# Pairwise complex sums with a lag of three, host-made masks and an FFN product in parts, in a Toeplitz-attention kernel on one core

## The chip, the cores and the metric

The kernel runs on one core of a Trainium2 chip. The metric is the device time of one execution in microseconds (us), lower is better. Before the change three runs gave 678.74, 679.80 and 680.02 us; their median, 679.8 us, is the time to beat. All data are float32.

The core has five instruction streams, each executed in its own order: TensorE (PE, matmuls; its weight loads are listed as PEld), VectorE (DVE), ScalarE (ACT), GpSimd (POOL) and SyncE (SP), which here only issues DMA transfers.

## The reference, cut to what matters

`x` has shape (4, 2048, 256). Two residual blocks follow one another.

```python
# block 1: gated Toeplitz operator
n  = layernorm(x)
u, v = split(silu(n @ uv_w), 2)              # 256 channels each
a  = rpe(lags) * 0.99 ** abs(lags)           # 4-layer network of width 32, one value per lag and channel
y  = irfft(rfft(a) * rfft(v))[:, :2048]      # convolution along the 2048 positions
x  = x + (u * y) @ o_w
# block 2: grouped linear layers without a nonlinearity between them
h1 = einsum('gmh,goh->gmo', layernorm(x).reshape(8, 1024, 256), W1) + b1
x  = x + einsum('gmo,gho->gmh', h1, W2) + b2 # 8 groups of 1024 tokens
```

## The kernel before, in words

**The convolution.** The long convolution of 4096 points is split by polynomial remainders into 8 rings, `r = 0` to 7. One *unit* is one batch `b` and one half `h` of 128 channels; there are 8 units. For each unit, `prepare` (L515, `split_real` and `split_complex`) forms the eight remainders from `c` by VectorE additions. `stage_b` (L545) then runs over the rings:

- `forward(r)` (L556) loads a 256 KB matrix (`ring_mats`), transforms the remainder by four 128x256 matmuls into the PSUM tile `pf`, and multiplies it as complex numbers by the kernel's transform `am`: `y = pf * a` (L574), `far = swapped pf * a2` (L576), then real parts subtracted (L577) and imaginary parts added (L578). The last two read two SBUF tiles; each covers 128 partitions by 256 elements.
- `backward(r)` (L580) loads the matrix of the way back and multiplies `y` into the PSUM tile `acc` (L591).
- `after(r)` (L597) combines the rings, two at a time.

`step(r)` (L679) does `forward(r)` and then `backward` and `after` of ring `r - LAG`, with LAG = 2, so that a unit takes 10 steps. `y` has three buffers of 128x512, `far` one, `pf` and `acc` two PSUM buffers each. Between the steps the main loop (L739) interleaves pieces of other work: `end()` of the previous unit (the last additions, the four sums `tk` of L674 and the multiplications by the gate on GpSimd, L676), `prepare` of the next unit from step 5 on, and, by `between`, whole stages of the neighbouring work.

**The other stages.** `stage_a(b, q)` (L254) normalizes and transposes 512 tokens, multiplies by `uv_w` and lets GpSimd build `c` (L274, L276). `gate` (L537) computes `u`. `stage_d(b, q)` (L689) multiplies by `o_w` (`po`, L697), adds to `x` (L699), normalizes, multiplies by the FFN matrix (`pff`, L715), adds (L717) and stores. Since the two FFN layers have nothing between them, `stage_w(g)` (L480) multiplies the two weight matrices of group `g` into one 256x256 matrix: four chunks of two 256 KB loads each, through two buffers for each matrix (WB = 2), a bias put in by ScalarE (L498), 16 matmul instructions into `pw` (L502), and one VectorE instruction for `wt` (L510). The groups 0 to 3 are formed before the units, 4 to 6 in one call after step 1 of the units (2,0), (2,1) and (3,0), and group 7 after the last unit.

**The start.** `rpe_network` (L299) evaluates the small network on all lags at once with block-diagonal weights. Its masks are made on the chip: `blk` (which of four blocks a partition belongs to) is a VectorE reduction of the identity matrix (L310), the block-diagonal weights `bd` (L317, three instructions) and the first layer's weights `w0` (L321) are products with `blk` and with a corner of the identity. The first matmul of the network (L332) needs `w0` and the row `lag_t`. Each layer goes PE (`ph`), ACT (square and copy), PE (variance, L341), DVE (`inverse_root`, nine to twelve small instructions, then L347), PE (transposes, L350), DVE (L351), ACT (L353). Then `rpe_transform` makes the transforms `am` (matmuls `hp` L453 and `pa` L458).

**What sets the order.** The kernel is written in a framework that traces the calls as written, gives each instruction a priority by that order, and then fixes one order for each engine by itself, from priorities, data dependences and free buffers; it also places the semaphores. An edit can thus move instructions that it doesn't name. Both builds' orders can be listed engine by engine.

Of the kernel before, what the change touches and what calls it, by code (L numbers as in the profile page):

```python
# [42 lines left out]
F, L = 32, 3  # L43
# [4 lines left out]
NR = 7  # L48
WB = 2
PIECES = 3  # L50
LAG = 2
WT = 4
D_STEPS = ((4, 0), (5, 1), (5, 0), (6, 2), (6, 1), (7, 3), (7, 2), (8, 3))
PI = 3.141592653589793
# [7 lines left out]
def kernel(  # L62
# [41 lines left out]
    am_d = const.tile([P, 2, 3, 2, P], F32, name="amd")  # L104
    am_c = [const.tile([P, 2, 2, 2, P], F32, name=f"am{r}") for r in range(NR)]

    BUFS = {"f4": 2, "f2": 2, "ring": 6, "y": 3, "far": 1, "i4": 4, "i2": 5}

    def t4(name, tag):
        return work.tile([P, 8 * P], F32, tag=tag, bufs=BUFS[tag], name=name)  # L110

    def t2(name, tag):
        return work.tile([P, 4 * P], F32, tag=tag, bufs=BUFS[tag], name=name)

    def load_x(b, q, tag):
# [181 lines left out]
        return t, y  # L297

    def rpe_network():  # L299
        par = t4("par", "f4")[:, : 2 * (L + 1) + (L + 1) * F]  # L300
        nc.sync.dma_start(par, rpe_par)
        lnw, lnb = par[:, 0 : L + 1], par[:, L + 1 : 2 * L + 2]
        fcw = par[:, 2 * L + 2 :].rearrange("p (l f) -> p l f", f=F)
        lag_t = t4("lag_t", "i4")
        nc.sync.dma_start(lag_t[0:4, :], lag_rows)
        early.update({(0, q): load_x(0, q, "xa") for q in range(2)})
        decay = t4("decay", "f4")[:, :NT]
        nc.sync.dma_start(decay, decays)
        blk = const.tile([P, 4], F32, name="blk")
        V.tensor_reduce(blk, ident.rearrange("p (s f) -> p s f", f=F), AX.X, ALU.add)  # L310
        mean = small.tile([P, L + 1], F32, tag="rmean", name="rmean")
        V.tensor_reduce(mean, fcw, AX.X, ALU.add)
        V.tensor_scalar_mul(mean, mean, 1.0 / F)
        V.tensor_tensor(fcw, fcw, mean[:, :, None].to_broadcast([P, L + 1, F]), ALU.subtract)
        bd = t2("bd", "f2")[:, : L * 4 * F].rearrange("p (l s f) -> p l s f", l=L, f=F)
        for i in range(L):
            V.tensor_tensor(  # L317
                bd[:, i], fcw[:, i : i + 1, :].to_broadcast([P, 4, F]), blk[:, :, None].to_broadcast([P, 4, F]), ALU.mult
            )
        w0 = t2("w0", "f2")[0:4, : 4 * F].rearrange("p (s f) -> p s f", f=F)  # L320
        V.tensor_tensor(  # L321
            w0, fcw[0:4, L : L + 1, :].to_broadcast([4, 4, F]), ident[0:4, 0:4, None].to_broadcast([4, 4, F]), ALU.mult
        )
        V.tensor_scalar_mul(blk, blk, 1.0 / F)

        zs = [None, None]
        for i in range(L + 1):
            sqs, ds = [], []
            for k in range(2):
                ph = ps_f.tile([P, 4 * P], F32, tag="pf", name=f"ph{i}_{k}")  # L330
                if i == 0:
                    T.matmul(ph, w0.rearrange("p s f -> p (s f)"), lag_t[0:4, k * 4 * P : (k + 1) * 4 * P], start=True, stop=True)  # L332
                else:
                    T.matmul(ph, bd[:, i - 1].rearrange("p s f -> p (s f)"), zs[k], start=True, stop=True)
                sqs.append(t2(f"sq{i}_{k}", "i2"))
                A.activation(sqs[k], ph, AF.Square)
                ds.append(t2(f"d{i}_{k}", "y"))
                A.copy(ds[k], ph)
            pv = ps_i.tile([P, 8, 4], F32, tag="acc", name=f"pvar{i}")
            for c in range(8):  # L340
                T.matmul(pv[:, c, :], sqs[c // 4][:, c % 4 * P : (c % 4 + 1) * P], blk, start=True, stop=True)  # L341
            t, y = inverse_root(pv.rearrange("p c s -> p (c s)"), NT, f"{i}")
            for k in range(2):

                e = t2(f"ne{i}_{k}", "i2")
                t_, y_ = (a[:, k * 16 : (k + 1) * 16, None].to_broadcast([P, 16, F]) for a in (t, y))
                V.scalar_tensor_tensor(e.rearrange("p (n f) -> p n f", f=F), t_, 1.5, y_, ALU.add, ALU.mult)  # L347
                pr = ps_i.tile([P, 4 * P], F32, tag="acc", name=f"pr{i}_{k}")
                for c in range(4):
                    T.transpose(pr[:, c * P : (c + 1) * P], e[:, c * P : (c + 1) * P], ident)  # L350
                V.tensor_tensor(ds[k], ds[k], pr, ALU.mult)  # L351
                zs[k] = t2(f"z{i}_{k}", "i2")
                A.activation(zs[k], ds[k], AF.Silu, bias=lnb[:, i : i + 1], scale=lnw[:, i : i + 1])  # L353
# [125 lines left out]

    def stage_w(g):  # L480
        na, oc = INTER // P, 2

        b1t = small.tile([P, 3, na], F32, tag="b1", bufs=2, name=f"b1_{g}")
        nc.sync.dma_start(b1t, b1[g])
# [7 lines left out]
        for o in range(0, na, oc):  # L492
# [6 lines left out]
            for m in range(2):  # L499
                for a in range(oc):  # L500
# [5 lines left out]
                        start=(o + a + m == 0),  # L506
                        stop=(o + a == na - 1 and m == 1),
                    )
        wt = wts[g] = tok.tile([P, 2, D], F32, tag="wt", bufs=WT, name=f"wt_{g}")
        V.scalar_tensor_tensor(wt, row[:, None, :].to_broadcast([P, 2, D]), 0.5, pw, ALU.mult, ALU.add)  # L510

# [32 lines left out]

    def stage_b(b, h):  # L545
        rs = rings[b, h]
        ys, accs = {}, {}
        nm = f"{b}_{h}"

        def i4(name):  # L550
# [5 lines left out]
        def forward(r):  # L556
            m = ring_mats(r, 0, f"{nm}_{r}")
            pf = ps_f.tile([P, 2, 2, P], F32, tag="pf", name=f"pf_{nm}_{r}")
            for k in range(2):
                cols = slice(k * P, (k + 1) * P)  # L560
                for xx in range(2):
                    if r == 0:
                        T.matmul(pf[:, k, xx, :], m[:, xx, cols], rs[r][:, k, xx, :], start=True, stop=True)
                    else:
                        T.matmul(pf[:, k], m[:, xx, cols], rs[r][:, :, xx, :], start=(xx == 0), stop=(xx == 1))  # L565
            y = ys[r] = t2(f"y_{nm}_{r}", "y").rearrange("p (k r c) -> p k r c", k=2, r=2)
            f = t2(f"far_{nm}_{r}", "far").rearrange("p (k r c) -> p k r c", k=2, r=2)
            if r == 0:
                a = am_d[:, h]
                V.tensor_tensor(y, pf, a[:, 0:2].rearrange("p r k c -> p k r c"), ALU.mult)  # L570
# [3 lines left out]
                V.tensor_tensor(y, pf, a[:, 0, :, None, :].to_broadcast([P, 2, 2, P]), ALU.mult)  # L574
                a2 = a[:, 1]
            V.tensor_tensor(f, pf[:, :, ::-1, :], a2[:, :, None, :].to_broadcast([P, 2, 2, P]), ALU.mult)  # L576
            V.tensor_tensor(y[:, :, 0, :], y[:, :, 0, :], f[:, :, 0, :], ALU.subtract)  # L577
            V.tensor_tensor(y[:, :, 1, :], y[:, :, 1, :], f[:, :, 1, :], ALU.add)  # L578

        def backward(r):  # L580
            m, y = ring_mats(r, 1, f"{nm}_{r}"), ys.pop(r)
# [6 lines left out]
            else:  # L588
                for c in range(2):
                    for k in range(2):  # L590
                        T.matmul(  # L591
                            acc[:, c].rearrange("p x c -> p (x c)"), y[:, k, c, :], m[:, k, :], start=(k == 0), stop=(k == 1)
                        )

        st = {}

        def after(r):  # L597
            acc = accs.pop(r)
# [126 lines left out]
    z = rpe_network()  # L725
    for q in range(NQ):
        stage_a(0, q)
    stage_w(0)
    stage_w(1)
    for h in range(2):  # L730
        gate(0, h)
    phs = load_phases()
# [1 line left out]
    for _ in prepare(0, 0):  # L734
        pass
    for g in range(2, WT):
        stage_w(g)
    end = None
    for b in range(B):  # L739
        for h in range(2):  # L740
# [10 lines left out]
                for q in range(NQ):  # L751
                    between[1 + q].append(lambda b=b, q=q: stage_a(b + 1, q))
            if WT <= 2 * b + h < 2 * B - 1:
                between[1].append(lambda g=2 * b + h: stage_w(g))
            queue = [end()] if end else []
            nxt = 2 * b + h + 1
            for r in range(NR + 1 + LAG):
# [9 lines left out]
    gate(B - 1, 1)  # L767
    for _ in end():
        pass
    stage_w(2 * B - 1)  # L770
    quarters = [stage_d(B - 1, q) for q in range(NQ)]
    for q in range(NQ + 1):
        if q < NQ:
# [104 lines left out]
```

## Time and profile before

| what | value |
|---|---|
| median of three runs | 679.8 us |
| the profiled execution, its own time | 680.03 us |
| its span, first to last instruction | 678.2 us (1.8 us lie around it) |
| mean granted TensorE clock | 0.975 |
| PE busy | 595.7 us, 88% |
| PEld busy | 463.1 us, 68% |
| DVE busy | 522.1 us, 77%, 1164 instructions |
| ACT busy | 303.4 us, 45% |
| POOL busy | 163.7 us, 24% |
| DMA | 81.36 MB, mean 120 GB/s |
| chain that ended last | DVE 35%, PE 34%, ACT 12%, DMA 7%, POOL 6% |

How to read it: the busy shares are averages over stages that have different limits, so the page alone doesn't say what one stage is worth. The profile can be cut into windows of time, in which each engine's busy time is listed (a window in which one engine is busy all the time is set by that engine), and it lists for each instruction the start, the duration, and the idle time of its engine just before it with the event that ended it. Units of the main loop can be found by their first forward matmuls (L563): 114.7, 211.5, 428.5 and 577.8 us are some of them. From the batch 1 on one batch takes 147 us (345 to 492 us is one such stretch).

### The profile page before, as it was taken

The page shows a single profiled execution, that of the slowest core. Times are in us where ns is not written, and L with a number is a line of the kernel's source. Part 1 is how long each engine was busy: PE and PEld are TensorE (multiplying, and loading weights), DVE is VectorE, ACT ScalarE, POOL GpSimd, SP SyncE. Part 2 cuts the span into 40 slices and gives each one's busy share as a digit, 9 for nine tenths or more (in the row PEclk, how much of TensorE's full clock was granted, in tenths as well). Part 3 has the DMA queues.
Part 4 walks back from the last instruction along what each step waited for, and adds up shares of the span by engine and source line. Part 5 has one row for each costly group of instructions (what it writes and reads, how often), then busy time and mean ns, then how long its engine had stood idle before and what let it go on. Part 6 is the DMA issues. An engine that isn't in the chain of part 4 may idle for free.

```text
span 678.2 us, 8266 instructions
## 1 busy us (share of the span) xinstructions
PE 595.7 (88%) x2620; PEld 463.1 (68%) x2620; DVE 522.1 (77%) x1164; ACT 303.4 (45%) x774; POOL 163.7 (24%) x186
## 2 busy tenths in 40 slices
PE   3989898899898789998997799898995999999897
PEld 1767455788677677765786687756784777766676
DVE  3554794579988998884469998981399999898854
ACT  3677641213341226668811155768711066511143
POOL 2333010001562231015521420134410311130310
PEclk9999999899898899999998999998999899999899
DMA  8423734664232523441245423431345223431202
GB/s 257 155 86 93 178 101 150 167 211 149 89 125 81 181 82 114 127 171 63 78 140 155 125 63 124 149 139 37 119 136 174 64 86 138 147 124 32 62 33 93
DMA packets 39988, 81.36 MB, mean 120 GB/s; under 512 B 5636, under 2 KB 7172, under 8 KB 39944
## 3 DMA queue, kind: packets, MB, share of 16 engines
q1 hardware_dynamic: 39208, 79.91, 38.2%
q10 hardware_dynamic: 736, 0.92, 0.4%
q8 instruction: 21, 0.34, 0.2%
q14 instruction: 23, 0.19, 0.1%
HBM read 72.42 MB, written 8.39 MB: 119 GB/s over the span
## 4 chain that ended last, share of the span: by engine, by line
DVE 35%; PE 34%; ACT 12%; DMA 7%; POOL 6%; issue 5%; SPq 0%; POOLq 0%; DVEq 0%; ACTq 0%
PE acc L591 6%; PE pff L715 5%; DMA w<-in_L_ffn_W_dram 5%; PE pf L565 4%; PE pw L502 4%; PE pv L268 4%; ACT junk_d L138 3%; DVE far L576 3%; ACT xn_d L161 2%; DVE y L574 2%; PE pa L458 2%; DVE tk L674 2%; PE pu L542 2%; DVE y L578 2%; POOL rs_d L140 2%
## 5 line engine op out<-in xcount | busy, mean ns | idle before, releaser
L591 PE MATMUL acc<-mats,y 128*128 128x256 f32 x448 | 107.8, 380 | 1.9 <-issue 1.2
L591 PEld LDWEIGHTS acc<-mats,y 128*128 128x128 f32 x448 | 84.0, 190 | 14.7 <-issue 2.4
L502 PE MATMUL pw<-w,w 128*128 128x256 f32 x256 | 70.9, 422 | 20.4 <-DMA w<-in_L_ffn_W_dram 19.4
L502 PEld LDWEIGHTS pw<-w,w 128*128 128x128 f32 x256 | 52.1, 211 | 34.9 <-ACT w L498 19.4
L676 POOL TENSOR_TENSOR gt<-gt,tk 128x512 f32<-128x512 f32 x32 | 47.4, 1505 | 110.3 <-DVE tk L674 100.9
L498 ACT ACTIVATE w<-w,dw 128x256 f32<-128x256 f32 x64 | 29.2, 500 | 92.7 <-DMA w<-in_L_ffn_W_dram 90.4
L697 PE MATMUL po<-ow,gt 128*128 128x256 f32 x256 | 61.3, 385 | 5.0 <-POOL gt L676 5.0
L268 PE MATMUL pv<-uvw,xnt 128*128 128x256 f32 x256 | 62.9, 396 | 2.1 <-ACT xnt L174 2.0
L565 PE MATMUL pf<-ra,mats 128*128 128x256 f32 x256 | 62.5, 380 | 1.2 <-PE acc L591 1.2
L715 PE MATMUL pff<-wt,xn 128*128 128x256 f32 x256 | 59.6, 383 | 1.3 <-ACT xn L172 1.3
L268 PEld LDWEIGHTS pv<-uvw,xnt 128*128 128x128 f32 x256 | 48.9, 197 | 13.1 <-ACT xnt L174 6.4
L697 PEld LDWEIGHTS po<-ow,gt 128*128 128x128 f32 x256 | 48.5, 193 | 13.7 <-POOL gt L676 7.4
L542 PE MATMUL pu<-xnt,uvw 128*128 128x512 f32 x128 | 56.7, 592 | 0.0
L715 PEld LDWEIGHTS pff<-wt,xn 128*128 128x128 f32 x256 | 47.4, 190 | 10.3 <-ACT xn L172 3.7
L615 ACT COPY e<-acc 128x512 f32<-128x512 f32 x24 | 13.9, 580 | 88.9 <-PE acc L591 54.6
L565 PEld LDWEIGHTS pf<-ra,mats 128*128 128x128 f32 x256 | 47.5, 190 | 7.7 <-PE acc L591 1.9
L274 POOL TENSOR_TENSOR c<-v 128x256 f32<-128x256 f32 x32 | 33.1, 1033 | 78.8 <-ACT v L269 78.8
L574 DVE TENSOR_TENSOR y<-pf,am 128x512 f32<-128x512 f32 x56 | 38.3, 684 | 9.5 <-PE pf L565 9.5
L161 ACT ACTIVATE xn_d<-xd,nb_d,rs_d 128x256 f32<-128x256 f32 x56 | 29.1, 590 | 32.5 <-POOL nb_d L142 21.2
L542 PEld LDWEIGHTS pu<-xnt,uvw 128*128 128x128 f32 x128 | 24.2, 190 | 25.9 <-issue 23.0
L140 POOL TENSOR_TENSOR rs_d<-ve_d,mhalf 128x4 f32<-128x4 f32 x12 | 14.1, 1173 | 112.2 <-DVE ve_d L139 112.2
L565 PE MATMUL pf<-rb,mats 128*128 128x256 f32 x128 | 35.2, 413 | 6.0 <-issue 5.1
(198 smaller groups left out, 1141.3 us busy)
## 6 DMA issues: line engine op xcount, KB each, us to landing
mats<-in_mats_dram SPq DMA_DIRECT2D x128, 256.0 KB, 2.7
w<-in_L_ffn_W_dram SPq DMA_DIRECT2D x64, 256.0 KB, 4.4
xa<-in_x_dram SPq DMA_DIRECT2D x18, 512.0 KB, 3.3
xd<-in_x_dram SPq DMA_DIRECT2D x14, 512.0 KB, 3.5
out_dram<-xd SPq DMA_DIRECT2D x12, 512.0 KB, 2.6
mats_rpe<-in_mats_dram SPq DMA_DIRECT2D x8, 256.0 KB, 3.7
row<-in_L_ffn_b_dram SPq DMA_DIRECT2D x8, 128.0 KB, 4.5
ph<-in_phases_dram SPq DMA_DIRECT2D x4, 256.0 KB, 6.1
```

What stands on the lines that cost most here:

```text
L161: A.activation(xn[:, i, :], xt[:, t, :], AF.Identity, bias=nb[:, t : t + 1], scale=rstd[:, t : t + 1])
L268: T.matmul(pv[:, hf, :], xnt[:, dt, o : o + P], uvw[:, dt, D:], start=(dt == 0), stop=(dt == 1))
L274: G.tensor_tensor(c[:, r, j0 : j0 + 2, 0, :], hi, lo, ALU.add)
L498: A.activation(w1s[:, a, :], w1s[:, a, :], AF.Identity, bias=d[:, o + a : o + a + 1])
L502: T.matmul(pw[:, m, :], w1s[:, a, m * P : (m + 1) * P], w2s[:, a, :], start=(o + a + m == 0), stop=(o + a == na - 1 and m == 1),)
L542: T.matmul(pu, uvw[:, dt, h * P : (h + 1) * P], xnts[b, q][:, dt, :], start=(dt == 0), stop=(dt == 1))
L565: T.matmul(pf[:, k], m[:, xx, cols], rs[r][:, :, xx, :], start=(xx == 0), stop=(xx == 1))
L574: V.tensor_tensor(y, pf, a[:, 0, :, None, :].to_broadcast([P, 2, 2, P]), ALU.mult)
L591: T.matmul(acc[:, c].rearrange("p x c -> p (x c)"), y[:, k, c, :], m[:, k, :], start=(k == 0), stop=(k == 1))
L676: G.tensor_tensor(gs, gs, tk, ALU.mult)
L697: T.matmul(po[:, i, :], gts[b, h][:, 2 * q + j, i, :], ow[:, h, :], start=(h == 0), stop=(h == 1))
L715: T.matmul(pf[:, i, :], xn2[:, dt, o : o + P], wt[:, dt, :], start=(dt == 0), stop=(dt == 1))
```

## The change

1. **Sums by pairs.** `y` and `far` become tiles for two rings (128x1024). The products of an even ring go to the first half, those of the odd ring to the second; only after the odd ring one subtraction and one addition, of 512 elements each, do the sums of both. `y` has two such pair buffers in place of three single ones, `far` one.
2. **A lag of three.** LAG goes from 2 to 3, so that `backward(r)` comes a step later and a unit has 11 steps.
3. **Masks from the host.** `blk` and the corner of the identity come as 8 more columns of the parameter array `par`; the reduction L310 goes, and `w0` is made ahead of `bd`.
4. **The FFN product in parts.** `stage_w` becomes a generator. For the groups 4 to 6 its four chunks follow after the steps 1 to 4 and `wt` after step 5. For the other groups all parts are still run at once.

```diff
-LAG = 2
+LAG = 3
...
-    BUFS = {"f4": 2, "f2": 2, "ring": 6, "y": 3, "far": 1, "i4": 4, "i2": 5}
+    BUFS = {"f4": 2, "f2": 2, "ring": 6, "y": 2, "far": 1, "i4": 4, "i2": 5}
...
     def t2(name, tag):
+        if tag in ("y", "far"):
+            return t4(name, tag)[:, : 4 * P]
...
     def rpe_network():
-        par = t4("par", "f4")[:, : 2 * (L + 1) + (L + 1) * F]
+        nw = 2 * (L + 1) + (L + 1) * F
+        par = t4("par", "f4")[:, : nw + 8]
...
-        blk = const.tile([P, 4], F32, name="blk")
-        V.tensor_reduce(blk, ident.rearrange("p (s f) -> p s f", f=F), AX.X, ALU.add)
+
+        blk, seg = par[:, nw : nw + 4], par[:, nw + 4 :]
         mean = small.tile([P, L + 1], F32, tag="rmean", name="rmean")
...
+        w0 = t2("w0", "f2")[0:4, : 4 * F].rearrange("p (s f) -> p s f", f=F)
+        V.tensor_tensor(
+            w0, fcw[0:4, L : L + 1, :].to_broadcast([4, 4, F]), seg[0:4, :, None].to_broadcast([4, 4, F]), ALU.mult
+        )
         bd = t2("bd", "f2")[:, : L * 4 * F].rearrange("p (l s f) -> p l s f", l=L, f=F)
...
-        w0 = t2("w0", "f2")[0:4, : 4 * F].rearrange("p (s f) -> p s f", f=F)
-        V.tensor_tensor(
-            w0, fcw[0:4, L : L + 1, :].to_broadcast([4, 4, F]), ident[0:4, 0:4, None].to_broadcast([4, 4, F]), ALU.mult
-        )
...
     def stage_w(g):
         na, oc = INTER // P, 2
+        yield
...
                         stop=(o + a == na - 1 and m == 1),
                     )
+            yield
         wt = wts[g] = tok.tile([P, 2, D], F32, tag="wt", bufs=WT, name=f"wt_{g}")
...
     def stage_b(b, h):
...
-            y = ys[r] = t2(f"y_{nm}_{r}", "y").rearrange("p (k r c) -> p k r c", k=2, r=2)
-            f = t2(f"far_{nm}_{r}", "far").rearrange("p (k r c) -> p k r c", k=2, r=2)
+
+            if r % 2 == 0:
+                st["y"], st["f"] = (
+                    t4(f"{t}_{nm}_{r}", t).rearrange("p (n k r c) -> p n k r c", n=2, k=2, r=2) for t in ("y", "far")
+                )
+            ypair, fpair = st["y"], st["f"]
+            y, f = ypair[:, r % 2], fpair[:, r % 2]
+            ys[r] = y
...
-            V.tensor_tensor(y[:, :, 0, :], y[:, :, 0, :], f[:, :, 0, :], ALU.subtract)
-            V.tensor_tensor(y[:, :, 1, :], y[:, :, 1, :], f[:, :, 1, :], ALU.add)
+            if r % 2:
+                for part, op in ((0, ALU.subtract), (1, ALU.add)):
+                    yp = ypair[:, :, :, part, :].rearrange("p n k c -> p (n k) c")
+                    fp = fpair[:, :, :, part, :].rearrange("p n k c -> p (n k) c")
+                    V.tensor_tensor(yp, yp, fp, op)
...
             if WT <= 2 * b + h < 2 * B - 1:
-                between[1].append(lambda g=2 * b + h: stage_w(g))
+                w = stage_w(2 * b + h)
+                for r in range(6):
+                    between[r].append(lambda w=w: next(w, 0))
...
-    inputs = {**inputs, "rpe_par": np.tile(par, (4, 1))}
+    eye = np.eye(P, 4)
+    inputs = {**inputs, "rpe_par": np.concatenate([np.tile(par, (4, 1)), np.repeat(np.eye(4), F, axis=0), eye], axis=1).astype(par.dtype)}
```

More of the change, by code (lines that the diff above doesn't have):

```diff
@@ L299, in rpe_network @@
     def rpe_network():
-        par = t4("par", "f4")[:, : 2 * (L + 1) + (L + 1) * F]
+        nw = 2 * (L + 1) + (L + 1) * F
+        par = t4("par", "f4")[:, : nw + 8]
         nc.sync.dma_start(par, rpe_par)
         lnw, lnb = par[:, 0 : L + 1], par[:, L + 1 : 2 * L + 2]
-        fcw = par[:, 2 * L + 2 :].rearrange("p (l f) -> p l f", f=F)
+        fcw = par[:, 2 * L + 2 : nw].rearrange("p (l f) -> p l f", f=F)
         lag_t = t4("lag_t", "i4")
@@ L546, in stage_b @@
         rs = rings[b, h]
-        ys, accs = {}, {}
+        ys, accs, st = {}, {}, {}
         nm = f"{b}_{h}"
@@ L593, in backward @@
                         )
-        st = {}
         def after(r):
@@ L727 @@
         stage_a(0, q)
-    stage_w(0)
-    stage_w(1)
+    for g in range(2):
+        list(stage_w(g))
     for h in range(2):
@@ L736 @@
     for g in range(2, WT):
-        stage_w(g)
+        list(stage_w(g))
     end = None
@@ L769 @@
         pass
-    stage_w(2 * B - 1)
+    list(stage_w(2 * B - 1))
     quarters = [stage_d(B - 1, q) for q in range(NQ)]
```

## The prediction

> **What bounds the kernel now.** I read the page's busy rows first (PE 88%, DVE 77%, so neither alone), then cut one batch into windows. Columns: window, its length, then busy us of PE, PEld, DVE, ACT, POOL.
>
> ```profile
> 206.70:245.30 38.60, 30.52 (x130) 25.07 (x129) 38.60 (x73) 5.18 (x11) 10.46 (x8) 0.91 0.46 136
> 245.30:292.00 46.70, 43.16 (x210) 35.98 (x208) 42.75 (x94) 29.18 (x87) 8.70 (x10) 1.00 0.36 114
> 345.00:391.00 46.00, 37.56 (x164) 30.96 (x163) 46.00 (x97) 5.54 (x12) 13.02 (x8) 0.93 0.48 138
> 391.00:458.00 67.00, 62.91 (x277) 47.44 (x276) 61.29 (x126) 42.70 (x125) 14.58 (x15) 1.00 0.36 120
> 458.00:492.00 34.00, 30.77 (x139) 23.74 (x138) 8.37 (x18) 26.23 (x71) 14.88 (x22) 0.95 0.23 78
> ```
>
> From the first `st` of a batch to the last `tk` (345 to 391 us) VectorE is busy 46.00 of 46.00: it alone sets that stretch. From there to the gate's end PE is busy 62.91 of 67 and VectorE 61.29: PE leads, with about 4 us of waits. Then 34 us of PE and ACT in which VectorE does 8 us. So a VectorE saving counts in the first stretch, little in the second, nothing in the third.
>
> The timeline of the first 24 us, VectorE, then PE:
>
> ```profile
> 4.08 0.29 DVE L314 TENSOR_TENSOR par<-par,rmean 128x128 f32<-128x128 f32 x1
> 6.99 0.76 DVE L147 BATCH_NORM_STATS2 st_a<-xa 128x6 f32<-128x256 f32 x2 [2.62 <-DMA xa<-in_x_dram]
> ...
> 9.37 0.27 DVE L310 TENSOR_REDUCE blk<-ident 128x4 f32<-128x128 f32 x1
> ...
> 10.42 0.69 DVE L317 TENSOR_TENSOR bd<-par,blk 128x128 f32<-128x128 f32 x3
> 11.03 0.28 DVE L321 TENSOR_TENSOR w<-par,ident 4x128 f32<-4x128 f32 x1
> ```
> ```profile
> 11.36 3.78 PE L332 MATMUL ph<-lag_t,w 4*128 4x512 f32 x4 [11.36 <-DMA w<-in_L_ffn_W_dram]
> 15.07 1.87 PE L341 MATMUL pvar<-blk,sq 128*128 128x4 f32 x8
> 16.80 1.52 PE L170 MATMUL pt_a<-ident,xn_a 128*128 128x128 f32 x6
> 18.11 1.71 PE L341 MATMUL pvar<-blk,sq 128*128 128x4 f32 x8
> 19.68 0.67 PE L170 MATMUL pt_a<-ident,xn_a 128*128 128x128 f32 x2
> ```
>
> PE does nothing for 11.36 us. The row names a weight load, but `ph` doesn't read it: it reads `w0`, which ends at 11.31. VectorE idles from 4.37 to 6.99 and makes `w0` only after the statistics of two `xa` tiles. From 11.36 on PE is busy 8.99 of 8.99 and then 42.96 of 45.65 us (to 66).
>
> **The masks.** The reduction (0.27) goes; 8 columns (4 KB on 68 KB) cost nothing. In the changed build's VectorE order `w0` stands fourth, right after L314: it ends at 4.37 + 0.3 = 4.7. The other operand, `lag_t`, was issued at 1.2; the loads behind it show that it has landed by 5.7. So `ph` starts at 5.0 to 5.7, and `ph` and `pvar` (3.78 + 3.4 us) end at 12.2 to 12.9, just as the normalized tokens come (ACT L161, 10.53 to 12.61). The first eight transposes (2 us) end near 14.6, in place of 20.35: a lead of 5.7 us. The matmuls are the same, and PE is nearly full afterwards, so most of it lasts. What could eat it: ScalarE now squares `ph` before it normalizes (two pairs of 0.6 us behind the end of `ph` at 8.8 to 9.5, done by 10.7, covered), PE has less other work between the transposes of layer one, and from 58 us the w ring, two buffers with 4.4 us a load, sets the pace: the chain of waits has weight loads at 66.00 and 74.33. A load is released by the matmuls before it, so the ring shifts as a whole; the changed PE order ends the second chunk about 1 us of matmul work later. From below 0, from above 7; I take 5.0, near what the timeline gives.
>
> **The sums.** The rows of the adds, all shapes apart:
>
> ```profile
> L578 DVE TENSOR_TENSOR y<-y,far 128x256 f32<-128x256 f32 x64 | 35.2, 550 | 0.0
> ...
> L577 DVE TENSOR_TENSOR y<-y,far 128x256 f32<-128x256 f32 x64 | 31.1, 486 | 0.3
> ```
>
> 128 instructions of 256 elements become 64 of 512. Back to back the timeline shows a start every 0.334 us for 256 elements (L577 to L578, 360.93 and 361.26) and every 0.600 us for 512. A merged one saves 2 x 0.334 - 0.600 = 0.068 us: 64 x 0.068 = 4.3 us, over all stages. [...]
>
> The means of 486 and 550 against medians of 418 and 419 are waits for GpSimd, 12.8 us together:
>
> ```profile
> 387.84 0.42 DVE L609 TENSOR_TENSOR s<-td,acc 128x256 f32<-128x256 f32 x1
> 388.17 0.57 DVE L577 TENSOR_TENSOR y<-y,far 128x256 f32<-128x256 f32 x1
> 388.66 1.48 DVE L578 TENSOR_TENSOR y<-y,far 128x256 f32<-128x256 f32 x1
> 390.07 0.41 DVE L610 TENSOR_TENSOR s<-td,acc 128x256 f32<-128x256 f32 x1
> ```
>
> GpSimd's gate product runs from 386.87 to 389.86; the add that reads PSUM (L609) passes, the two that read SBUF twice wait. [...] by the rows it is the adds that wait. In the new order one pair of adds still stands right behind the first two `tk`, the other pair some 3.8 us behind the second two, past the product. I take a gain of 1.5 us; ends -3 (a loss) and +6.
>
> **The lag and the order.** I added up the spacings along both builds' VectorE orders. From a batch's first `st` to its last `tk` the work falls from 35.8 to 33.6, 45.0 to 42.6 and 45.6 to 42.6 us, 7.7 in all: the block behind `after(3)` moves past it. PE pays part back. From the first `po` that needs the second gate to the gate's end its order holds 67.9 in place of 66.6 us (one `backward`, 1.73, now comes after that point), +1.3; the third time the end is another, and I take the same; +0.4 in the stage after it. So 7.7 - 3 x 1.7 = 2.6 us. The moved `po` additions may let the 4 us of waits of the second stretch shrink; that is inside the range. The units (0,0) and (0,1): 0.5 us. Against: after the last unit's seventh product two backwards instead of one are left, and the new PE order puts 2.1 us more before the last `acc`, on the chain of `end`, GpSimd and `po` that closes at 640.8: +1.6 us.
>
> **Buffers.** A pair buffer is written again when both its backwards are done: `y(4)` waits for `acc(1)`, `y(6)` for `acc(3)`, which PE has behind `po` batches (3.2 us). Behind it on VectorE wait sums and the `xd` additions that `po` and the normalization need. In the 46 us stretch PE is ahead (37.56 of 46), in the next PE is the bound anyway. Taken at 0; up to 1.73 to 4.9 us a time.
>
> **FFN parts.** The same 48 matmul instructions and 24 loads. PE now stands still up to 4 us for a load (370.87: 4.08; 224.87: 3.69), but inside the stretch that VectorE fills: covered, 0. If VectorE no longer covered it, it would be about 4 us three times. On SP the loads stand among ring matrices; with three buffers each these are early. Ends -2 and +3.
>
> **Sum.** 5.0 + 1.5 + 2.6 + 0.5 - 1.6 = 8.0, and 0.3 of plain spacing gain in other VectorE-bound stretches: 8.3. The profiled execution took 680.03 us (span 678.2 and 1.8 around it), 0.2 above the median: 680.0 - 8.3 = 671.7, for the median 671.5 us.
>
> **Rivals.** (A) The w ring keeps its own time and the head start is lost: 679.8 - 3.3 = 676.5. For it: two of the start's waits on the chain are weight loads. Against: they are released by PE's own matmuls. (B) A head start of 7, all 7.7 us of VectorE without PE paying, and 2 us of the second stretch's waits gone: 679.8 - 7 - 7.7 - 2 - 0.5 + 1.6 = 664.2. Against: PE is 94% busy there. (C) Slower: the pair buffers. 16 times (`y(4)` and `y(6)` in eight units) VectorE stands for a backward that PE has behind `po`. At 1 us each it costs 16 and gives 679.8 + 16 - 8.3 = 687.5; it decides from 8.3 / 16 = 0.5 us each. Against: PE has slack where VectorE is the bound.
>
> **Chances.** Main case 0.57, its own range 667.5 to 675; A 0.20, of which 0.05 ends within 0.2% of before (1.4 us, about what a measurement of this kernel can tell from no change); B 0.15; C 0.08. Faster 0.57 + 0.15 + 0.15 = 0.87, same 0.05, slower 0.08. The range 665 to 678.5 leaves out C, the best of B and the end of A.
>
> **What would show it.** Right: `ph` at 5 to 5.7 us, `hp` near 85 instead of 90.14; 64 adds of 128x512 with a median near 690 ns; the stretch from `st` to the last `tk` shorter by 2 to 3 us with VectorE still full; the next one not shorter than 66. Wrong: `hp` still at 90 (A); idle before L574's successor with `acc` as releaser (C); PE waits below 2 us in the second stretch (B).

## The result and the profile after

The changed kernel takes 675.86 us, median of 15 runs (673.67 to 680.34), against 679.8 us before (15 runs beside them): ratio 0.9938, 95% interval 0.9917 to 0.9958, a gain of 4.2 us (2.9 to 5.6) where 8.3 were foretold. Its profiled execution took 674.42 us with a span of 672.6 us; before it was 678.2, so 5.6 us separate the two traces. The mean granted TensorE clock (the share of its full clock that TensorE gets) is 0.975 in both traces; over all 15 runs of the changed kernel it is 0.971, over the 30 runs of the kernel before that stand beside the first experiments 0.979.

The start is as foretold. Timeline of the first microseconds after, PE and then VectorE:

```profile
5.64 3.75 PE L335 MATMUL ph<-lag_t,w 4*128 4x512 f32 x4 [5.64 <-DVE par L327]
9.32 3.58 PE L344 MATMUL pvar<-par,sq 128*128 128x4 f32 x16
12.75 1.95 PE L172 MATMUL pt_a<-ident,xn_a 128*128 128x128 f32 x8
```
```profile
4.18 0.29 DVE L317 TENSOR_TENSOR par<-par,rmean 128x128 f32<-128x128 f32 x1
4.51 0.28 DVE L319 TENSOR_TENSOR w<-par 4x128 f32<-4x128 f32 x1
```

`w0` ends at 4.79 and `ph` starts at 5.64; the first eight transposes are done at 14.7. `hp` starts at 84.3 us (90.1 before).

Next, the stages of the loop. Windows after, then the one window of before that the prediction did not show (length, busy us of PE, PEld, DVE, ACT, POOL, then the clock, the DMA share and GB/s):

```profile
199.80:236.90 37.10, 28.08 (x124) 22.29 (x123) 37.10 (x65) 4.59 (x11) 7.41 (x9) 0.95 0.48 135
236.90:304.40 67.50, 63.46 (x276) 47.75 (x275) 53.67 (x113) 45.58 (x134) 13.71 (x14) 1.00 0.37 123
304.40:340.80 36.40, 30.38 (x148) 25.14 (x146) 12.86 (x24) 24.27 (x65) 17.17 (x23) 0.95 0.26 82
340.80:386.60 45.80, 37.02 (x158) 30.03 (x157) 45.65 (x89) 4.74 (x10) 7.16 (x9) 0.89 0.42 126
386.60:453.70 67.10, 63.27 (x277) 47.83 (x276) 54.77 (x116) 45.55 (x134) 14.16 (x14) 1.00 0.35 120
453.70:488.60 34.90, 29.79 (x144) 24.17 (x142) 11.81 (x22) 23.93 (x64) 17.48 (x23) 0.95 0.23 78
```
```profile
312.00:344.90 32.90, 29.05 (x138) 22.68 (x137) 8.09 (x18) 26.07 (x71) 14.61 (x21) 1.00 0.24 80
```

VectorE still fills the first stretch (37.10 of 37.10; 45.65 of 45.80), but the third, from the gate's end to the next `st`, has grown from 32.90 to 36.40 us, and VectorE's work in it from 8.09 to 12.86.

Cutting every trace at the same events (first `st` of a batch, end of its last `tk`, end of the gate's matmuls `pu`) gives the ledger. V is the stretch from `st` to the last `tk`, G from there to the gate's end, A from there to the next `st`; the number counts the batch. Each row is one profiled execution, in us:

| kernel | to first V | V1 | G1 | A1 | V2 | G2 | A2 | V3 | G3 | rest |
|---|---|---|---|---|---|---|---|---|---|---|
| before | 206.7 | 39.3 | 66.0 | 32.9 | 47.4 | 66.0 | 33.7 | 48.1 | 59.5 | 78.6 |
| after | 199.8 | 37.1 | 67.5 | 36.4 | 45.8 | 67.1 | 34.9 | 46.6 | 59.2 | 78.2 |
| difference | -6.9 | -2.2 | +1.5 | +3.5 | -1.6 | +1.1 | +1.2 | -1.5 | -0.3 | -0.4 |

In these two traces 6.9 us come from the start, 5.3 from the three stretches that VectorE fills, and 7.0 go back in the stages G and A. The ledger holds the clock too: in A1 it was 1.00 before and is 0.95 after (the last section shows the dip). PE's idle time in A1 goes from 3.9 to 6.0 us and in A2 from 3.2 to 5.1, so 4.0 of the 4.7 us that A grows are waits.

What is late in A1 stands in VectorE's timeline after. Where before goes from `ve_a` of the third quarter (325.87) straight to the ring products and has the last quarter's `nm_a` at 331.94 after waiting for ScalarE,

```profile
325.87 0.17 DVE L139 TENSOR_SCALAR ve_a<-acc_a 128x4 f32<-128x4 f32 x1 [2.91 <-ACT junk_a L138]
...
331.94 0.17 DVE L136 TENSOR_SCALAR nm_a<-acc_a 128x4 f32<-128x4 f32 x1 [2.05 <-ACT junk_a L134]
```

after has:

```profile
317.85 0.69 DVE L585 TENSOR_TENSOR y<-pf,am 128x512 f32<-128x512 f32 x1 [2.65 <-PE pf L570]
318.46 0.68 DVE L587 TENSOR_TENSOR far<-pf,am 128x512 f32<-128x512 f32 x1
319.18 2.00 DVE L592 TENSOR_TENSOR y<-y,far 128x512 f32<-128x512 f32 x2
321.10 0.41 DVE L615 TENSOR_TENSOR td<-acc,ed 128x256 f32<-128x256 f32 x1
321.43 0.41 DVE L616 TENSOR_TENSOR td<-acc,ed 128x256 f32<-128x256 f32 x1
321.76 1.84 DVE L686 TENSOR_TENSOR tk<-p 128x512 f32<-128x512 f32 x2
323.52 1.23 DVE L138 TENSOR_SCALAR nm_a<-acc_a 128x4 f32<-128x4 f32 x1
```

`nm_a` is a product of 4 elements in each partition that opens the last quarter's normalization. ScalarE had its input ready at 322.3; it now stands behind two `tk`, and itself takes 1.23 us in place of 0.17, while GpSimd runs the products of these `tk` (323.07 to 325.95). Behind it come ScalarE's squares, `rs_a` on GpSimd (behind those products and four `c`), the normalization, and PE:

```profile
323.07 2.88 POOL L688 TENSOR_TENSOR gt<-gt,tk 128x512 f32<-128x512 f32 x2 [0.63 <-DVE tk L686]
...
329.31 1.03 POOL L142 TENSOR_TENSOR rs_a<-ve_a,mhalf 128x4 f32<-128x4 f32 x1
```

```profile
331.31 0.93 PE L172 MATMUL pt_a<-ident,xn_a 128*128 128x128 f32 x4 [3.11 <-ACT xn_a L163]
```

PE stands still for 3.11 us in a stage in which VectorE is idle for 23.5 of 36.4 us: what counts is not how much VectorE has to do there, but what stands ahead of a small instruction, here of `nm_a` on VectorE and of `rs_a` on GpSimd.

The sums, by shape:

```profile
L592 DVE TENSOR_TENSOR y<-y,far 128x512 f32<-128x512 f32 x64 | 49.6, 813 | 0.2
```

64 of 128x512, with a median of 684 ns; the mean of 813 holds 64 x 0.129 = 8.3 us over it, read as waits for GpSimd, less than the 12.8 before. In the trace after, the 48 of these adds that no product of GpSimd (`gt` or `c`) overlaps take at most 0.69 us, the 16 others 0.69 to 1.75. Before, 101 of the 128 adds of 256 elements run alone and take at most 0.43 us, the 27 others 0.41 to 1.49. The adds of `td` and `acc`, which read PSUM, show no such waits: 12 before and 30 after run beside a product, and the longest takes 0.425 us, as the longest alone does.

### The profile page after: what moved, and what is told of

Read it like the earlier page. It is cut to its first block, busy times and chain, and to the rows that moved or that the text cites. A ratio compares the mean times of both kernels' runs of the same rounds, so it can differ in the third digit from the quotient of the medians.

```text
span 672.6 us, 8173 instructions
## 1 busy us (share of the span) xinstructions
PE 592.9 (88%) x2620; PEld 462.4 (69%) x2620; DVE 511.8 (76%) x1099; ACT 304.3 (45%) x774; POOL 152.7 (23%) x186
## 4 chain that ended last, share of the span: by engine, by line
PE 39%; DVE 30%; ACT 12%; POOL 7%; DMA 7%; issue 4%; SPq 0%; POOLq 0%; DVEq 0%; ACTq 0%
PE acc L605 7%; DMA w<-in_L_ffn_W_dram 6%; PE pf L570 5%; PE pff L727 5%; PE pw L506 5%; PE pu L547 4%; PE pv L270 4%; DVE y L592 3%; PE po L709 2%; ACT xn_d L163 2%; PE pa L461 2%; DVE far L587 2%; POOL rs_d L142 2%; DVE y L585 2%; ACT junk_d L140 2%
## 5 line engine op out<-in xcount | busy, mean ns | idle before, releaser
L506 PE MATMUL pw<-w,w 128*128 128x256 f32 x256 | 66.5, 406 | 12.9 <-DMA w<-in_L_ffn_W_dram 12.0
L506 PEld LDWEIGHTS pw<-w,w 128*128 128x128 f32 x256 | 50.4, 204 | 26.5 <-ACT w L502 15.1
L585 DVE TENSOR_TENSOR y<-pf,am 128x512 f32<-128x512 f32 x56 | 38.3, 683 | 26.9 <-PE pf L570 23.7
L570 PEld LDWEIGHTS pf<-ra,mats 128*128 128x128 f32 x256 | 48.2, 193 | 10.2 <-issue 4.4
L727 PEld LDWEIGHTS pff<-wt,xn 128*128 128x128 f32 x256 | 47.5, 190 | 10.7 <-ACT xn L174 4.3
L570 PE MATMUL pf<-rb,mats 128*128 128x256 f32 x128 | 38.1, 433 | 13.5 <-DVE far L587 7.3
L592 DVE TENSOR_TENSOR y<-y,far 128x512 f32<-128x512 f32 x64 | 49.6, 813 | 0.2
L276 POOL TENSOR_TENSOR c<-v 128x256 f32<-128x256 f32 x32 | 27.4, 857 | 91.9 <-ACT v L271 91.9
L163 ACT ACTIVATE xn_d<-xd,nb_d,rs_d 128x256 f32<-128x256 f32 x56 | 29.1, 590 | 34.8 <-POOL nb_d L144 23.7
```

Source lines behind the costliest of these rows:

```text
L163: A.activation(xn[:, i, :], xt[:, t, :], AF.Identity, bias=nb[:, t : t + 1], scale=rstd[:, t : t + 1])
L506: T.matmul(pw[:, m, :], w1s[:, a, m * P : (m + 1) * P], w2s[:, a, :], start=(o + a + m == 0), stop=(o + a == na - 1 and m == 1),)
L592: V.tensor_tensor(yp, yp, fp, op)
L727: T.matmul(pf[:, i, :], xn2[:, dt, o : o + P], wt[:, dt, :], start=(dt == 0), stop=(dt == 1))
```

## The experiments

Ratios are to the kernel before, run beside each kernel, with 95% intervals; 0.001 is 0.68 us. The clock is the mean granted clock over all runs of the kernel; of the kernel before it was 0.978 or 0.979 beside each group of experiments.

| kernel | median us | ratio | interval | clock |
|---|---|---|---|---|
| the changed kernel | 675.9 | 0.9938 | 0.9917 to 0.9958 | 0.971 |
| masks only | 674.2 | 0.9892 | 0.9862 to 0.9921 | 0.981 |
| masks and parts | 673.1 | 0.9869 | 0.9834 to 0.9904 | 0.981 |
| masks and lag 3 | 672.2 | 0.9871 | 0.9835 to 0.9908 | 0.981 |
| masks, lag 3 and parts | 676.3 | 0.9931 | 0.9909 to 0.9953 | 0.979 |
| changed, without masks | 683.6 | 1.0034 | 1.0016 to 1.0052 | 0.971 |
| changed, without parts | 677.1 | 0.9937 | 0.9912 to 0.9963 | 0.972 |
| changed, lag 2 | 703.3 | 1.0323 | 1.0286 to 1.0360 | 0.958 |
| changed, 4 pieces a step | 684.2 | 1.0051 | 1.0030 to 1.0071 | 0.969 |
| changed, 4 pieces in second units | 678.1 | 0.9950 | 0.9929 to 0.9971 | 0.972 |
| changed, sums at once | 685.4 | 1.0081 | 1.0055 to 1.0106 | 0.969 |
| changed, late sums in small instructions | 683.1 | 1.0024 | 1.0002 to 1.0047 | 0.972 |
| changed, three pair buffers | 672.4 | 0.9865 | 0.9831 to 0.9898 | 0.983 |

**The masks alone** (the diff's part 3 on the kernel before).

> The kernel before with the masks from the host alone (8 more columns, w0 ahead of bd); sums, lag and FFN products as before. The trace after shows ph at 5.64 instead of 11.36, hp at 84.3 instead of 90.1, and at the end of the span 5.6 us less. Main theory: the head start of 5.8 us lasts to the end and the other three parts together are worth about nothing, so this kernel takes 679.8 - 5.8 = 674 us (673 to 675.5), not slower than the whole change (675.9). Rival: the lead wears away behind loads of weights and ring matrices, and what is left at the end comes from the sums; then 677.5 to 680.

674.2 us, as the main theory had it: the whole gain of the change and perhaps more. Its trace has `ph` at 5.7, `hp` at 84.8, and from there the stages of before (A1 32.9, A2 32.8). The lead of 6 us is still there at the end; the w ring did not eat it.

**The rest alone** (the changed kernel with part 3 taken back).

> The changed kernel with its masks made on the chip as before; pair sums, lag 3 and parts stay. Theory: the three other parts together are worth nothing or a small loss, 679.8 to 682.5, and hp starts near 90. Rival, by the prediction's sum (1.5 + 2.6 + 0.5 - 1.6 + 0.3 = 3.3 us): 676.5.

683.6 us, ratio 1.0034: pair sums, lag and parts together cost 2.3 us (1.1 to 3.5). The masks are worth 0.0034 + 0.0062 = 0.0096, 6.5 us, within the changed kernel. The rival, which was the prediction's own sum of 3.3 us gained, falls.

**Lag 2 under the pair sums.**

```diff
-LAG = 3
+LAG = 2
```

> The changed kernel with a lag of 2 instead of 3; pair sums, masks and parts stay. Main theory: it is the lag that puts the second two tk of batch 1's and 2's first units between the statistics of the last quarters of stage_a, which cost 3.5 and 1.2 us after the gate; with a lag of 2 the four tk stand 1 instruction apart in VectorE's order again, so these 4.7 us come back, while the three VectorE stretches lose most of the 5.3 us that they had gained but also the 2.3 us that PE paid back: 675.9 - 4.7 + 5.3 - 2.3 = 674.2, taken as 672.5 to 675; the stretch from the gate's end to the next st is near 33 instead of 36.4 us. Rival: the pair sums themselves cost the time there (two adds took 2.0 us against GpSimd): the stretch stays at 36 us and the kernel at 676 to 679.

703.3 us: both theories missed. The pair sums need the third step of lag. By the code, an even ring's sum waits for its partner, and with a lag of 2 its `backward` is due in the very next step after that. The trace doesn't show that step as a wait (PE waits for `y` for 0.8 us in all); what PE waits for is the normalization of stage_d, `xn_d`, 23.7 us against 11.4, so how the one leads to the other stays open. V and G grow, G most:

```profile
243.30:315.70 72.40, 64.92 (x273) 49.05 (x273) 51.68 (x107) 45.19 (x132) 12.87 (x12) 0.95 0.34 108
402.20:473.60 71.40, 63.50 (x269) 47.53 (x268) 51.69 (x107) 45.23 (x132) 12.82 (x12) 0.98 0.34 109
```

72.40 and 71.40 in place of 67.5 and 67.1, with PE idle for 7.5 and 7.9 us in place of 4.0 and 3.8; the rest goes with the clock, 0.95 and 0.98 in place of 1.00. The lag is not an edit beside the pair sums but the price of entry: without it they cost another 26 us.

**Lag 3 without pair sums** (masks, LAG = 3, sums as before, four single `y` buffers).

> The masks from the host and a lag of 3, with the sums still ring by ring (four single y buffers, far 128x512) and the FFN products in one call. What the lag does by itself. Theory now: the lag alone moves the second two tk of a batch's first unit behind the statistics of the third quarter and ahead of those of the fourth (VectorE order: 16 instructions apart instead of 1), so the stretch from the gate's end to the next st grows from 32.9 to 35 us or more in batches 1 and 2, and the kernel takes 676 to 679, against 674.2 of the masks alone. Rival: the lag by itself costs nothing, it is the pair sums (two adds of 1 us behind the products, against GpSimd) that lengthen the stretch: then 33 us there and 673 to 675 in all.

The stage came as the theory said, the time did not:

```profile
305.90:341.00 35.10, 29.29 (x150) 24.45 (x149) 15.47 (x29) 24.89 (x67) 16.75 (x22) 1.00 0.28 91
341.00:386.30 45.30, 35.74 (x154) 29.00 (x153) 45.27 (x92) 5.64 (x12) 12.35 (x9) 0.94 0.47 134
453.40:490.20 36.80, 30.96 (x150) 25.61 (x149) 15.50 (x29) 24.90 (x67) 16.74 (x22) 0.95 0.29 86
```

A grows to 35.10 and 36.80 (masks only: 32.9 and 32.8) and PE's idle time in it from 3.8 to 5.8, with no pair sum in the kernel; VectorE has 15.5 us of work there in place of 8.1. In its order the same two `tk` stand ahead of the last quarter's `nm_a`. But V2 falls to 45.30 from 47.5. The lag moves VectorE work out of V into A and G; the gain in V that the prediction gave to the change is this move. In sum 672.2 us, a difference to the masks alone of -1.4 us (+-3), which can't be told from none.

**Four pieces of other work after each step.**

```diff
-PIECES = 3
+PIECES = 4
```

> The changed kernel with 4 instead of 3 pieces of other work after each step. In VectorE's order the last three tk of each unit then stand together, early, and no tk is left between the statistics of the later quarters of stage_a. Main theory: the loss of 3.5 and 1.2 us in the two stage_a stretches goes, and little else changes: 675.9 - 4 = 672 (671 to 673.5). Rival (the pair sums, or the products of the forward step themselves, delay the statistics): 675 to 677.

```profile
308.70:341.40 32.70, 28.94 (x145) 23.46 (x143) 8.64 (x21) 25.79 (x71) 13.50 (x21) 1.00 0.26 89
463.30:495.90 32.60, 28.87 (x144) 23.39 (x143) 8.55 (x20) 25.78 (x71) 13.41 (x21) 1.00 0.27 90
```

With the `tk` gone from it, A is back at 32.70 and 32.60, as the theory had it. The kernel is slower all the same (684.2): V1 falls to 34.0, and G rises to 73.6 and 74.5, with PE idle for 7.9 and 8.6 us in place of 4.0 and 3.8. What is late there is the normalization of stage_d: PE's waits for `xn_d` are 19.7 us in all, 11.4 in the changed kernel.

**Four pieces only in the second units.**

```diff
-            for _ in range(PIECES if ...
+            for _ in range((PIECES + (h == 1 and b + 1 < B)) if ...
```

> The changed kernel with 4 instead of 3 pieces of other work after each step, but only in the second unit of batches 0 to 2, in which stage_a of the next batch runs; the first units keep 3. With 4 in every unit the stretch from the gate's end to the next st fell to 32.7 and 32.6 us (36.4 and 34.9 in the changed kernel), and the stage_d stretch before it grew by 6. Theory: the loss there is the second two tk that stand on VectorE, and their products on GpSimd, ahead of the last quarter's statistics; here they are gone and stage_d is left as it is: 675.9 - 3.7 - 2.3 = 670 (669 to 672). Rival: the four tk close together only move the wait into the stretch before (PE behind VectorE, statistics of the first quarter late): 674 to 677.

678.1 us: the theory's number fell. A1 is 32.1, but A2 stays at 34.9, V2 and V3 are 48.0 and 49.1 again, and G2 is 69.7 (with 3.8 us of PE idle time as in the changed kernel, at a clock of 0.98). In A2 the wait is still there although no `tk` stands ahead of the last quarter's `nm_a`, which takes its 0.17 us:

```profile
475.19 0.17 DVE L138 TENSOR_SCALAR nm_a<-acc_a 128x4 f32<-128x4 f32 x1 [1.98 <-ACT junk_a L136]
```
```profile
481.11 1.02 POOL L142 TENSOR_TENSOR rs_a<-ve_a,mhalf 128x4 f32<-128x4 f32 x1
```
```profile
483.10 1.18 PE L172 MATMUL pt_a<-ident,xn_a 128*128 128x128 f32 x4 [2.98 <-ACT xn_a L163]
```

`ve_a` ends at 479.13, but `rs_a` on GpSimd comes behind four `c` that GpSimd began at 478.38. So the `tk` are one cause of the late normalization and the order on GpSimd is another. I have no placement that keeps A short without giving V its work back.

**The parts**, taken out of the changed kernel, added to the masks, and added to masks and lag.

> The changed kernel with the FFN products of groups 4 to 6 in one call again. The main theory gives them nothing, as the stretch with the loss (batch 1, 304 to 341 us) holds none of their parts: 675.9, within 1.4. Rival: the parts, with their loads spread on SP and their PE work behind other products, cost 2 us or more: 674 or less. Other side: the parts saved the 4 us standstills for weight loads (VectorE was idle for moments in the second and third stretch): 677.5 or more.

> The masks from the host and the FFN products of groups 4 to 6 in parts; sums and lag as before. The changed kernel with and without parts took 675.9 and 677.1 us. Theory: the parts spread loads that PE waited for up to 4 us, but under a full VectorE, so they give nothing here: 674.2, within 1.4. Rival: the parts are worth 1.3 us or more by themselves, as in the pair kernels: 671.5 to 673, which would be the fastest kernel so far.

> The changed kernel without the pair sums only: masks, lag 3 and parts, each ring's sums right behind its products, four single y buffers. So far: masks alone 674.2, masks and parts 673.1, masks and lag 672.2; with pair sums too, 677.1 (without parts) and 675.9 (with). Theory: it is the pair sums that cost, some 4.5 us, so this takes 671 to 672.5 and beats the changed kernel by 4. Rival: the parts that differ are scatter between runs of some minutes, and the pair sums cost nothing: 674.5 to 677.

The first pair differs by 0.0001 in the ratio, the second by -0.0023 (+-0.0046), the third by +0.0060 (+-0.0043). The parts are worth nothing in the changed kernel, and of opposite signs elsewhere. The third difference lies at the end of the kernel: the two traces reach the last `tk` at 633.0 and 633.5 us, and behind it are 37.5 and 41.2. With the parts, 28 of the 32 `pw` matmuls that the trace lists for the last group are left for the stretch behind G3, without them 20; that group is not one of those in parts, so it is the framework's order that has moved them. The third expectation's theory (that the pair sums by themselves cost 4.5 us) fell where the parts are in: the kernel without pair sums is not faster than the changed one (0.9931 and 0.9938). Without the parts (0.9871 and 0.9937) they do cost 0.0066 (+-0.0045). What the pair sums are worth thus hangs on that order too, and the last three runs take it apart.

**Each ring's sums at once, in the pair buffers** (128 adds of 256, right behind the products).

> The changed kernel with its pair buffers (two y tiles of 128x1024, one far), but each ring's own subtraction and addition of 256 elements right behind its products, 128 instructions as before. It keeps the buffers' coarseness and takes away the wait of an even ring for its odd partner. If the pair sums cost by that wait (backward of an even ring can't start until its partner's products are done, and after the last unit's seventh ring two backwards are left): 671 to 673, and the stage from the last unit's products to the last tk falls from 40.7 to 38 us. If they cost by the coarser buffers (products waiting for the backward of the ring four before): 675 to 677, like the changed kernel.

**Late sums in small instructions** (after the odd ring, four adds of 256 in place of two of 512).

> The changed kernel with its sums still after the odd ring, but as four instructions of 256 elements instead of two of 512. The wait for the partner stays, the size goes. Spacings of before (0.334 us for 256 elements, 0.600 for 512) make it 64 x 0.068 = 4.3 us more VectorE work, of which a third to a half lies in stretches that VectorE sets: theory 677 to 679, slower than the changed kernel by 1.5 to 2.5. Rival: large adds lose more by being held up at GpSimd's products (813 ns mean against 690) than they save: 673 to 675.5.

The first takes 685.4 us, beyond both of its theories: against single buffers with the same sums (0.9931) the pair buffers cost 0.0150, 10.2 us (+-2.3). A1 and A2 are 39.3 and 38.8, with PE idle for 8.3 and 7.5. The second takes 683.1 us, so that merging small late sums into large ones saves 0.0086, 5.8 us (+-2.1), more than either theory had. The same pair of rings in the two traces, small ones first:

```profile
142.00 1.42 DVE L591 TENSOR_TENSOR y<-y,far 128x256 f32<-128x256 f32 x4
```
```profile
142.24 1.28 DVE L592 TENSOR_TENSOR y<-y,far 128x512 f32<-128x512 f32 x2
```

Four small ones take 1.42 us and two large ones 1.28: 0.14 for each pair, 4.4 us for 32 pairs, as the spacing said. Busy time of VectorE falls from 517.5 to 511.8, by 5.7. The clock is the same (0.972 and 0.971), so this difference owes nothing to it.

**Three pair buffers.**

```diff
-    BUFS = {... "y": 2, "far": 1, "i4": 4, "i2": 5}
+    BUFS = {... "y": 3, "far": 1, "i4": 4, "i2": 4}
```

> The changed kernel with three instead of two pair buffers for y; to make room, the small work tiles of tag i2 get four buffers instead of five. Pair buffers with the sums at once cost 9 us more than single buffers (685.4 against 676.3). If it is waiting for a pair to be read before it is written again, a third pair gives back 3 us or more: 671 to 673, and the two stretches from the gate's end to the next st fall below 35 us. If it is only the order that the framework makes of it, nothing is won: 675 to 678 (the missing i2 buffer can only add to it, so a time above 676 doesn't tell the two apart).

672.4 us, ratio 0.9865: 0.0073 below the changed kernel, 5.0 us (+-2.7), though one `i2` buffer is gone. The waits that go with it can be read in the changed kernel's trace, VectorE and then PE:

```profile
246.80 0.69 DVE L585 TENSOR_TENSOR y<-pf,am 128x512 f32<-128x512 f32 x1 [0.53 <-PE acc L605]
...
328.24 0.69 DVE L585 TENSOR_TENSOR y<-pf,am 128x512 f32<-128x512 f32 x1 [0.22 <-PE acc L605]
...
396.57 0.69 DVE L585 TENSOR_TENSOR y<-pf,am 128x512 f32<-128x512 f32 x1 [0.52 <-PE acc L605]
...
608.33 0.69 DVE L585 TENSOR_TENSOR y<-pf,am 128x512 f32<-128x512 f32 x1 [1.75 <-PE acc L605]
```
```profile
367.86 3.78 PE L570 MATMUL pf<-rb,mats 128*128 128x256 f32 x8 [3.50 <-DVE far L587]
```

A product waits for a `backward` four times, 3.0 us in all; the same four, within 0.01 us, stand in the kernels without masks and without parts (there with a fifth of 0.53), and none in this one. PE's waits of `pf` for `far` fall from 7.3 to 2.7 us; the one of 3.50 is gone, but it lay in V2, which VectorE fills. A:

```profile
308.60:342.70 34.10, 28.96 (x149) 24.14 (x147) 14.31 (x26) 24.16 (x65) 16.64 (x22) 1.00 0.29 93
```

34.10 and 34.1 in place of 36.4 and 34.9; V2 and V3 are both 44.9 (45.8 and 46.6). Little of this is waiting. PE's idle time in A is 5.1 and 5.1 us (6.0 and 5.1), and the rest of A's gain goes with the clock, 1.00 in place of 0.95. V2 is shorter since a pair of sums that stood behind `st` (1.81 us at 341.95) now stands ahead of it, in A, where VectorE is idle; V3 has the same move. So the third buffer changes the order and the clock as well as the waits, and that the waits are what the 5.0 us come from is not shown. This kernel, masks and parts, and masks and lag are the fastest; their intervals overlap, and each lies wholly below the changed kernel's.

## Why the prediction was right, and where not

**Masks: 5.0 foretold, 6.5 (+-1.9) measured.** The mechanism and its times held: `ph` 5.64 (5.0 to 5.7), transposes done at 14.7 (14.6), `hp` 84.3 (near 85); the `par` load with 8 columns more lands 2.9 us after its issue, 2.8 before. Rival A, the lead lost in the w ring, did not happen, although its number, 676.5, is the nearest of all. The masks are the whole gain.

**Spacing of the sums: right.** 0.068 us for each merged pair of instructions, against 0.070 (1.42 and 1.28 us for four and two); the durations of single adds (medians of 0.418 us for 256 elements before and 0.684 for 512 after), added up, would make it 0.30 for two merges, where the trace has 0.14. On the whole kernel the merging gives 5.8 us (+-2.1), about the 4.3 of the spacing and the 1.5 that I took for the waits for GpSimd; what the adds take over their median falls from 10.5 to 8.2 us between these two kernels. I had credited only 1.8 of it beside the 7.7 of the order.

**The lag: the step that failed is "+0.4 in the stage after it".** The prediction summed the spacings up to the last `tk` and found 7.7 us less work; the trace has 5.3 us. PE's payment in G, put at 1.3 a time, was 1.5, 1.1 and -0.3. But the stage A took 3.5 and 1.2 us, 4.7 in place of 0.8 (4.0 of it PE's waits), since I counted PE's work there and looked at VectorE only as an idle engine: "Then 34 us of PE and ACT in which VectorE does 8 us". The list of VectorE's order showed the two `tk` between the third and the fourth quarter's statistics, and I read it as moved work, not as a delay of `nm_a` and of GpSimd's `rs_a` behind their products. So 5.3 - 2.3 - 4.7 = -1.7: a loss in place of the gain of 2.6. That PE waits more in A with the lag does not hang on one trace: in A1 and A2 together it is idle for 11.0 to 11.6 us in the changed kernel, without masks, without parts, and in both kernels with the lag and single buffers, against 6.8 to 7.6 us in the three with single buffers and a lag of 2.

**Buffers: "taken at 0", and about 5 us.** This is rival C at a fraction of its price. Four waits, not sixteen, 0.75 us each at the mean, make 3.0 us; a third buffer gives back 5.0 us (+-2.7), with a higher clock and another order. The argument "PE has slack where VectorE is the bound" held inside V, where none of the four lies; they lie in G, A and the last unit. This and the lag's term overlap, since the third buffer also takes 0.9 us of PE's waits out of A1, so they are not to be added.

**Tail: 1.6 foretold as a cost, none found.** From the end of G3 the rest is 78.2 us (78.6): the last `tk` comes 2.4 us later after G3, but PE first works off `pw` of the last group, which ends 40.5 us after G3 (at 634.9) in place of 41.4 (at 641.0). The later `tk` is hidden behind that work, and the end behind the `tk` is 2.7 us shorter.

**Batch 0 and parts.** The units of batch 0 were put at 0.5; the lead grows from 5.8 at `hp` to 6.9 at the first V, 1.1 in one trace. The other kernels with the masks come to the first V at 200.0 to 203.7 us, a lead of 3.0 to 6.7, and the changed kernel without masks at 208.1, so these traces don't show a gain there. Parts: 0 foretold, 0 (+-2.3).

**The change as a whole.** The masks gave 6.5 and the other three parts took 2.3, where I had given them 3.3. That leaves 4.2, and the forecast of 8.3 was too high by the lag's and the buffers' terms. That the time fell inside the foretold range is the masks' doing alone; for the other three parts together the sign was wrong. The sum also has no term for the clock: against the masks alone the change loses 0.0046, 3.1 us (+-2.5), and its clock is 0.971 against 0.981. What isn't settled: how much of this is the clock, and how much of the 10.2 us that pair buffers cost with sums at once is waiting and how much is the other order that the framework makes of it. The trace there has direct waits of `y` for `acc` of only 1.1 us, and that kernel's clock is 0.969 against 0.979 with single buffers.

## What to carry to other kernels

Work that is moved out of a full stretch lands somewhere: before crediting the gain, look in the new order of each engine for the tiny instruction (a statistic, a scale) that now stands behind it, and follow that one to the engine that waits, even where the engine is idle most of the time. When buffers are made twice as large and fewer, price their release one by one and measure one buffer more; a third pair buffer gave 5.0 us here, more than any of the three edits beside the masks as a whole. And measure the parts of a bundle alone: the cheapest edit, 8 columns from the host, was the whole gain.

## What was not expected of the hardware

A VectorE instruction of 4 elements, `nm_a`, took 1.23 us when a GpSimd product of the gate was running (323.52 after, also 310.75 before). After, the nine of the twelve `nm_a` that no such product overlaps take 0.16 to 0.17 us, and the three others 0.63, 1.23 and 1.23: small as they are, they took up to seven times as long.

The granted clock of equal work differs between kernels. G1 of the changed kernel without parts took 69.2 us at a clock of 0.98 and that of the changed kernel 67.5 at 1.00, with the same 4.0 us of PE idle time, so the 1.7 us between them go with the clock. In eight traces (before, after, without parts, the two with the lag and single buffers, sums at once, late sums in small instructions, three pair buffers) it is 0.89 to 0.96 in the stretches V and 0.97 to 1.00 in G, and the mean over a profiled run goes from 0.955 (lag 2) to 0.982 (masks and lag). With one profile for each kernel, stage differences below 2 us are therefore read only where several kernels show them.

A lower mean clock is made of short dips. In the traces of before and after, the recorded clock is 1.00 or 0.50, and between the first 20 us and the last 4 each has eight stretches at 0.50, 34.1 us together: thirteen of the sixteen last 3.4 us, two 6.8 and one 10.2. In these stretches one 128x256 matmul starts 0.427 us after the one before it (median), outside 0.216. In A1 of the changed kernel (after the length comes PE's busy time; the clock stands third from the end):

```profile
325.40:332.40 7.00, 3.83 (x19) 2.89 (x19) 2.97 (x7) 3.92 (x11) 4.52 (x7) 1.00 0.29 75
332.40:335.80 3.40, 3.40 (x12) 2.67 (x11) 0.00 (x0) 1.39 (x3) 0.00 (x0) 0.50 0.47 154
```

The standstill of 3.11 us is followed by 3.4 us at half the clock, so by these spacings PE does 1.7 us less work there. In the 7 us ahead of each of the sixteen stretches PE was busy for 3.3 to 5.1 us, 47 to 72%, against 88% over either span. No run varied this by itself, so that the waits bring the dips is not shown, and not each wait has its dip: A1 of the kernel without parts has the same 6.0 us of PE idle time as that of the changed kernel, and a clock of 1.00.

The clock also divides the kernels. All eight with two pair buffers ran at means of 0.958 to 0.972, the others at 0.978 to 0.983. Over 111 runs of the kernel before, which all execute the same instructions, a straight line gives 3.9 us less for each 0.01 of clock (correlation -0.72). By that line, as an estimate, the 0.012 between two and three pair buffers are 4.6 us, of 5.0 measured, and the 0.009 between the masks alone and the change 3.6 us, of 3.1 measured; of the 10.2 us that the pair buffers cost with sums at once it makes 3.8. So the clock, which no term of the prediction held, could account for much of what the two pair buffers cost.
